# Pairwise products of 256 features: seven input places with refills and four output pieces per round, in place of a resident input and five

## The chip, the cores and the metric

One core of one Trainium2 chip. The metric is the device time of one execution in microseconds (us). The kernel before takes 1274.88 us, the median of 3 runs (1274.85 to 1274.91). The profile is of one execution, and its span (first to last instruction) is a little shorter, 1273.1 us.

## The reference

For every row of a batch of 4096 rows with 256 float32 features, all products of two features with i <= j are written, in the order of the upper triangle:

```python
# inputs: (4096, 256) float32
dot = jnp.einsum('bi,bj->bij', inputs, inputs)
iu, ju = jnp.triu_indices(256)
y = dot[:, iu, ju]            # (4096, 32896) float32
```

An output row has 256 x 257 / 2 = 32,896 columns, 131,584 bytes. The input is 4.19 MB, the output 538.97 MB. Row i of the triangle is a *run* of 256 - i columns: feature i times the features i to 255.

## The kernel before

128 partitions hold batch rows; a *round* is two batch rows per partition (256 rows in all), so there are 16 rounds. The whole input stays in SBUF (32 KB per partition). The columns of a round are cut into five pieces of about 6592 columns, each with an output buffer from a pool of three. ScalarE computes the first runs of a piece, one instruction per run and row; VectorE the others, both rows and often two neighbouring runs in one instruction. Two DMAs, one per row of the round, send the buffer out. The very first buffer goes out in four parts, so that the DMA gets work early.

```python
P = 128
UNIT = 64
REPEAT = 2
PIECES = 5
BUDGET = 0.95
FIRST = [512, 1536, 3584]
# ...
def vector_time(block: list) -> float:
    return sum(68 + 1.046 * REPEAT * n * m for (*_, n), m in vector_ops(block))
# ... split(): how many runs ScalarE takes, until VectorE's time is within BUDGET ns per element
    groups = n // (P * REPEAT)
    borders = even_borders(0, width, PIECES)
    slot = max(b - a for a, b in zip(borders, borders[1:]))

    xpool = ctx.enter_context(tc.tile_pool(name="x", bufs=1))
    opool = ctx.enter_context(tc.tile_pool(name="o", bufs=3))

    x_in = x.rearrange("(g p r) d -> p g (r d)", p=P, r=REPEAT)
    x_out = out.rearrange("(g p r) c -> g p r c", p=P, r=REPEAT)

    total = n // P * d
    xt = xpool.tile([P, total + 1], F32, name="x")
    nc.vector.memset(xt[:, total:], 0.0)
    cuts = [0, 1, groups // 2, groups]
    for a, b in zip(cuts, cuts[1:]):
        xs = xt[:, a * REPEAT * d : b * REPEAT * d]
        nc.sync.dma_start(xs.rearrange("p (g c) -> p g c", g=b - a), x_in[:, a:b])

    for g in range(groups):
        for c, (lo, hi) in enumerate(zip(borders, borders[1:])):
            o = opool.tile([P, REPEAT, slot], F32, tag="o", name=f"o_{g}_{c}")
            first = g == c == 0
            cuts = [lo, *(FIRST if first else []), hi]
            for a, b in zip(cuts, cuts[1:]):
                block = runs(d, a, b)
                k = split(block, 0.0 if first else BUDGET * REPEAT * (b - a))
                # ... ScalarE: block[:k], VectorE: block[k:]
                for r in range(REPEAT):
                    nc.sync.dma_start(x_out[g][:, r, a:b], o[:, r, a - lo : b - lo])
```

A VectorE instruction that takes two runs uses the length of the first for both, so its second run reads one element past its row: the first element of the next row in SBUF, which in the last row of a round belongs to the next round. What it writes there is overwritten by the next run.

In HBM, partition p of round g writes rows 256 g + 2 p and 256 g + 2 p + 1. Neighbouring partitions of one DMA are two rows apart.

Of the kernel before, what the change touches and what calls it, by code (L numbers as in the profile page):

```python
# [1 line left out]

# [4 lines left out]

F32 = mybir.dt.float32
AF = mybir.ActivationFunctionType
ALU = mybir.AluOpType  # L10

P = 128
UNIT = 64
REPEAT = 2
PIECES = 5
BUDGET = 0.95
FIRST = [512, 1536, 3584]


def even_borders(lo: int, hi: int, pieces: int) -> list[int]:  # L20
    units = (hi - lo) // UNIT
    return [lo + units * c // pieces * UNIT for c in range(pieces)] + [hi]


def runs(d: int, lo: int, hi: int) -> list:


    found, at = [], 0
    for i in range(d):
        a, b = max(at, lo), min(at + d - i, hi)  # L30
        if a < b:
            found.append((i, i + a - at, a, b - a))
        at += d - i
    return found


def vector_ops(block: list) -> list:

    ops, k = [], 0
    while k < len(block):
        i, j, at, n = block[k]
        m = 2 if k + 2 < len(block) and i == j else 1
        ops.append((block[k], m))
        k += m
    return ops


def interleave(block: list) -> list:


    half = len(block)
    while half and len(vector_ops(block[:half])) > len(vector_ops(block[half:])):
        half -= 1
    a, b = vector_ops(block[:half]), vector_ops(block[half:])
    return [op for k in range(max(len(a), len(b))) for ops in (a, b) for op in ops[k : k + 1]]


def vector_time(block: list) -> float:
    return sum(68 + 1.046 * REPEAT * n * m for (*_, n), m in vector_ops(block))


def split(block: list, budget: float) -> int:


    scalar, k = 0.0, 0
    while k < len(block):
        scalar += REPEAT * (184 + 0.837 * block[k][3])  # L70
        if vector_time(block[k:]) <= budget or scalar > vector_time(block[k + 1 :]):
            break
        k += 1
    return k


def window(ap: bass.AP, free: list) -> bass.AP:
    return bass.AP(ap.tensor, ap.offset, [list(ap.ap[0]), *free])


@with_exitstack
def kernel(
    ctx: ExitStack, tc: tile.TileContext, x: bass.AP, out: bass.AP
):

    nc = tc.nc  # L90
    n, d = x.shape
    width = out.shape[1]
    assert n % (P * REPEAT) == 0 and width == d * (d + 1) // 2 and width % UNIT == 0
# [4 lines that stand above are left out]
    xpool = ctx.enter_context(tc.tile_pool(name="x", bufs=1))  # L98
    opool = ctx.enter_context(tc.tile_pool(name="o", bufs=3))

    x_in = x.rearrange("(g p r) d -> p g (r d)", p=P, r=REPEAT)
    x_out = out.rearrange("(g p r) c -> g p r c", p=P, r=REPEAT)


    total = n // P * d
    xt = xpool.tile([P, total + 1], F32, name="x")
    nc.vector.memset(xt[:, total:], 0.0)  # L107
    cuts = [0, 1, groups // 2, groups]
    for a, b in zip(cuts, cuts[1:]):
        xs = xt[:, a * REPEAT * d : b * REPEAT * d]  # L110
        nc.sync.dma_start(xs.rearrange("p (g c) -> p g c", g=b - a), x_in[:, a:b])  # L111

    for g in range(groups):
        for c, (lo, hi) in enumerate(zip(borders, borders[1:])):
# [5 lines that stand above are left out]
                k = split(block, 0.0 if first else BUDGET * REPEAT * (b - a))  # L120
                for i, j, at, length in block[:k]:
                    for r in range(REPEAT):
                        row = (g * REPEAT + r) * d
                        nc.scalar.activation(  # L124
                            o[:, r, at - lo : at - lo + length],
                            xt[:, row + j : row + j + length],
                            AF.Copy,
                            scale=xt[:, row + i : row + i + 1],
                        )
                row = g * REPEAT * d  # L130
                for (i, j, at, length), m in interleave(block[k:]):
                    at -= lo
                    nc.vector.tensor_tensor(  # L133
                        o[:, :, at : at + m * length],
                        window(xt[:, row + j :], [[d, REPEAT], [1, m], [1, length]]),
                        window(xt[:, row + i :], [[d, REPEAT], [1, m], [0, length]]),
                        ALU.mult,
                    )
                for r in range(REPEAT):
                    nc.sync.dma_start(x_out[g][:, r, a:b], o[:, r, a - lo : b - lo])  # L140


# [1 line left out]
_INS = ["r_inputs"]  # L144
_OUTS = [((4096, 32896), "float32")]


# [20 lines left out]
```

## Time and profile before

| | |
|---|---|
| time | 1274.88 us (1274.85 to 1274.91) |
| span of the profiled execution | 1273.1 us |
| VectorE busy | 995.9 us (78%), 1813 instructions |
| ScalarE busy | 486.7 us (38%), 1547 instructions |
| DMA queue | 26,000 packets, 543.17 MB, 99.8% of 16 engines |
| output DMAs | 166, of which 128 have 3296 KB and 30 have 3264 KB |
| input DMAs | 3: 256, 1792 and 2048 KB |

A packet here is one partition's piece of one output row (up to 26,368 bytes) or one 2 KB stretch of input; each DMA also leaves one small completion packet on each of the 16 DMA engines. "Busy" of the DMA is the time that packets took, as a share of what 16 engines have in the span. An idle engine costs nothing if it is not the one that bounds the time.

### The profile page before, as it was taken

The numbers are of one execution on the slowest core, as the hardware profiler recorded it, in microseconds if no ns is written. First come the engines' busy times: TensorE is split into PE (matmuls) and PEld (weight loads), VectorE is DVE, ScalarE is ACT, GpSimd is POOL, SyncE is SP. The second block draws the span as 40 slices with busy tenths as digits, with TensorE's granted clock in tenths as the row PEclk, the third lists the DMA queues.
The fourth block names the chain that finished last, engine by engine and source line by source line (L and its number), as shares of the span: only waits on it lengthen the run. The fifth ranks groups of instructions, "written<-read, shape, count | busy, mean of one in ns | idle before, by whom it ended". The sixth has DMA issues, their size and how long they took to land.

```text
span 1273.1 us, 3975 instructions
## 1 busy us (share of the span) xinstructions
DVE 995.9 (78%) x1813; ACT 486.7 (38%) x1547; POOL 0.2 (0%) x4
## 2 busy tenths in 40 slices
DVE  8987887878778777787787787777777777777770
ACT  5523535234342343424334252342523425234250
POOL 0000000000000000000000000000000000000000
DMA  9999999999999999999999999999999999999998
GB/s 379 431 431 434 427 435 424 436 425 434 427 434 423 436 425 435 424 435 426 434 428 431 430 431 426 434 428 431 429 431 429 431 430 429 428 431 429 432 431 349
DMA packets 26031, 543.43 MB, mean 427 GB/s; under 512 B 2704, under 2 KB 2704, under 8 KB 5264
## 3 DMA queue, kind: packets, MB, share of 16 engines
q1 hardware_dynamic: 26000, 543.17, 99.8%
q14 instruction: 31, 0.25, 0.0%
HBM read 4.19 MB, written 538.97 MB: 427 GB/s over the span
## 4 chain that ended last, share of the span: by engine, by line
DMA 70%; DVE 25%; issue 1%; SPq 1%; DVEq 0%
DMA out_dram<-o 70%; DVE o L133 25%; SPq L140 1%; DMA x<-in_r_inputs_dram 1%; DVEq L133 0%; SPq L111 0%
## 5 line engine op out<-in xcount | busy, mean ns | idle before, releaser
L133 DVE TENSOR_TENSOR o<-x 128x356 f32<-128x356 f32 (+61 forms) x1812 | 995.8, 627 | 240.8 <-DMA out_dram<-o 191.4
L124 ACT ACTIVATE o<-x 128x253 f32<-128x253 f32 (+41 forms) x1546 | 485.4, 404 | 749.2 <-DMA out_dram<-o 722.3
L124 ACT ACT_TABLE_LOAD x1 | 1.3, 1283 | 0.7 <-PEq L155 0.7
L107 DVE MEMSET x<- 128x1 f32 x1 | 0.1, 59 | 0.8 <-PEq L155 0.8
L155 POOL MEMSET const-bfloat16-1.0<- 128x1 bf16 x1 | 0.1, 102 | 0.0
L155 POOL MEMSET const-uint8-127<- 128x1 uint8 x1 | 0.1, 102 | 0.0
L155 POOL MEMSET const-float32-0.0<- 128x1 f32 x1 | 0.1, 99 | 0.2 <-issue 0.2
L155 POOL MEMSET const-float32-1.0<- 128x1 f32 x1 | 0.1, 99 | 0.0
## 6 DMA issues: line engine op xcount, KB each, us to landing
out_dram<-o SPq DMA_DIRECT2D x128, 3296.0 KB, 27.2
out_dram<-o SPq DMA_DIRECT2D x30, 3264.0 KB, 28.8
out_dram<-o SPq DMA_DIRECT2D x2, 1472.0 KB, 13.0
x<-in_r_inputs_dram SPq DMA_DIRECT2D x1, 2048.0 KB, 13.4
out_dram<-o SPq DMA_DIRECT2D x2, 1024.0 KB, 9.7
x<-in_r_inputs_dram SPq DMA_DIRECT2D x1, 1792.0 KB, 8.2
out_dram<-o SPq DMA_DIRECT2D x2, 512.0 KB, 11.0
out_dram<-o SPq DMA_DIRECT2D x2, 256.0 KB, 10.5
```

Of the source, the lines that this page charges most:

```text
L107: nc.vector.memset(xt[:, total:], 0.0)
L124: nc.scalar.activation(o[:, r, at - lo : at - lo + length], xt[:, row + j : row + j + length], AF.Copy, scale=xt[:, row + i : row + i + 1],)
L133: nc.vector.tensor_tensor(o[:, :, at : at + m * length], window(xt[:, row + j :], [[d, REPEAT], [1, m], [1, length]]), window(xt[:, row + ...
L140: nc.sync.dma_start(x_out[g][:, r, a:b], o[:, r, a - lo : b - lo])
L155: nc = _bacc.Bacc("TRN2", target_bir_lowering=False, num_devices=1)
```

## The change

The partition now holds 32 adjacent batch rows of its own, in all rounds: partition p of round g has rows 32 p + 2 g and 32 p + 2 g + 1. Thus its input is one contiguous stretch per load. Only seven rounds have a place in SBUF at a time; after the first piece of rounds 3, 6 and 9, three more rounds are loaded into places whose rounds are done (at round 9 in two DMAs, as the places wrap around). The SBUF freed this way goes to the three output buffers, which grow from 6592 to 8224 columns, so that a round goes out in four pieces of 32,896 bytes per row. The unit of the cuts is 32 columns instead of 64, as 8224 is no multiple of 64. In HBM neighbouring partitions of one DMA are now 32 rows apart.

```diff
 P = 128
-UNIT = 64
+UNIT = 32
 REPEAT = 2
-PIECES = 5
+PIECES = 4
 BUDGET = 0.95
+AHEAD = 7
+LOADED = 3
 FIRST = [512, 1536, 3584]
@@
-    x_in = x.rearrange("(g p r) d -> p g (r d)", p=P, r=REPEAT)
-    x_out = out.rearrange("(g p r) c -> g p r c", p=P, r=REPEAT)
+    x_in = x.rearrange("(p r) d -> p (r d)", p=P)
+    x_out = out.rearrange("(p g r) c -> g p r c", p=P, r=REPEAT)
 
-    total = n // P * d
+    total = AHEAD * REPEAT * d
     xt = xpool.tile([P, total + 1], F32, name="x")
     nc.vector.memset(xt[:, total:], 0.0)
-    cuts = [0, 1, groups // 2, groups]
-    for a, b in zip(cuts, cuts[1:]):
-        xs = xt[:, a * REPEAT * d : b * REPEAT * d]
-        nc.sync.dma_start(xs.rearrange("p (g c) -> p g c", g=b - a), x_in[:, a:b])
+
+    def load(g: int, end: int):
+        while g < end:
+            place = g % AHEAD
+            m = min(end - g, AHEAD - place)
+            a, b, size = g * REPEAT * d, place * REPEAT * d, m * REPEAT * d
+            nc.sync.dma_start(xt[:, b : b + size], x_in[:, a : a + size])
+            g += m
+
+    load(0, 1)
+    load(1, AHEAD)
@@ (ScalarE and VectorE read the place of the round)
-                        row = (g * REPEAT + r) * d
+                        row = (g % AHEAD * REPEAT + r) * d
@@
-                row = g * REPEAT * d
+                row = g % AHEAD * REPEAT * d
@@ (after the two output DMAs of a piece)
+            if c == 0 and g and g % LOADED == 0 and g - LOADED + AHEAD < groups:
+                load(g - LOADED + AHEAD, min(g + AHEAD, groups))
```

## The prediction

> **What bounds the kernel now.** I read the page first: its slices, queues and chain.
>
> ```profile
> DMA  9999999999999999999999999999999999999998
> GB/s 379 431 431 434 427 435 424 436 425 434 427 434 423 436 425 435 424 435 426 434 428 431 430 431 426 434 428 431 429 431 429 431 430 429 428 431 429 432 431 349
> DMA packets 26031, 543.43 MB, mean 427 GB/s; under 512 B 2704, under 2 KB 2704, under 8 KB 5264
> ...
> q1 hardware_dynamic: 26000, 543.17, 99.8%
> ...
> DMA 70%; DVE 25%; issue 1%; SPq 1%; DVEq 0%
> ```
>
> The 16 DMA engines are busy 99.8% of the span and move about 430 GB/s in every slice but the first and the last. 543.17 MB at 430 GB/s is 1263 us of a span of 1273.1 us. The chain gives 25% to VectorE, but each of those stretches lies beside a full DMA queue, so I ask next who waits for whom.
>
> ```profile
> ACT o L124 <- DMA out_dram<-o: 722.3, 74, 12.7
> DVE o L133 <- DMA out_dram<-o: 191.4, 59, 4.0
> ```
>
> VectorE waits 191.4 us, in about 3 us pieces, for an output buffer to drain. One buffer takes it about 12.4 us (the chain in order of time) and takes the DMA 2 x 3296 KB / 430 GB/s = 15.7 us. Compute is ahead by 3.3 us per buffer; a faster VectorE buys nothing in the middle of the run. So the time is: the wait for the first packet, bytes and packets on the slowest DMA engine, any moment at which the DMA queue is empty, and the tail. The empty moments can only be at the start, so I looked at it in steps of 5 us and in order of time.
>
> ```profile
> 0.00:5.00 5.00, 1.40 (x5) 2.63 (x5) 0.20 (x4) 1.00 0.54 172
> 5.00:10.00 5.00, 3.57 (x8) 5.00 (x14) 0.00 (x0) 1.00 1.01 358
> 10.00:15.00 5.00, 5.00 (x7) 5.00 (x16) 0.00 (x0) 1.00 1.05 403
> 15.00:20.00 5.00, 5.00 (x7) 4.45 (x14) 0.00 (x0) 1.00 1.04 431
> 20.00:25.00 5.00, 5.00 (x6) 0.00 (x0) 0.00 (x0) 1.00 1.04 441
> 25.00:30.00 5.00, 5.00 (x8) 0.00 (x0) 0.00 (x0) 1.00 1.03 441
> ```
>
> The last two columns are the DMA share and GB/s. The DMA starts at about 2.1 us (issue at 0.73 us, so 1.4 us from issue to first packet) and is never empty again. This is not luck of the outputs alone: the queue holds all 4.19 MB of input first, some 11 us of work, and behind that cover the engines fill the first buffers.
>
> ```profile
> 3.66 4.28 DVE L133 TENSOR_TENSOR o<-x 128x512 f32<-128x512 f32 x9 [2.80 <-DMA x<-in_r_inputs_dram]
> 5.05 2.80 SPq L140 DMA_DIRECT2D out_dram<-o  x4
> 9.37 1.19 DVE L133 TENSOR_TENSOR o<-x 128x988 f32<-128x988 f32 x1 [1.43 <-DMA x<-in_r_inputs_dram]
> ...
> 12.55 1.09 SPq L140 DMA_DIRECT2D out_dram<-o  x2
> ...
> 15.74 1.07 SPq L140 DMA_DIRECT2D out_dram<-o  x2
> ...
> 28.03 0.81 SPq L140 DMA_DIRECT2D out_dram<-o  x2
> ```
>
> The first buffer goes out at 5.05 to 15.74 us in four parts, the second at 28.03 us. Bytes ahead of the second are 4.19 + 6.68 = 10.87 MB; with the measured rates they last until about 28.8 us. The cover is just long enough. At 9.37 us VectorE waits 1.43 us for the second input load: a product of two runs reads one element past its rows, the first of the next round.
>
> **What the Trainium skill says.** "DMA: Bandwidth & Descriptors", Where 436 GB/s comes from: 16 ports carry 435.2 GB/s. The trace's 430 is 99% of it, so larger pieces can win at most about 1%. Same page, Latency and other measured facts (row pitch): a pitch of 4 MiB between partitions halved the rate of copies, 4 MiB plus 4 KiB did not. The trace of before has a pitch of two rows, 263,168 bytes, at full rate; of a 4 MiB pitch no run here shows anything. Same page, How a descriptor splits into AXI transactions: a start off a 256-byte line costs part of one extra transaction. Same page, Queues, rings and completion order: each engine takes descriptors in ring order, so a refill waits behind the outputs issued before it and delays the later ones by its own length.
>
> **The change part by part.**
>
> 1. *Fewer, longer output packets.* The packet records of the trace have medians of 84 ns for 2048 bytes, 159 for 4096, 309 for 8192, 441 for 11,776, 973 for 26,112 and 981 for 26,368. The line through the 8192 and 26,368 bytes has 0.0370 ns per byte; what is not proportional to bytes is 6 to 14 ns a packet, depending on whether the median, the mean (983.7 ns) or the page's port rate is taken. I choose 11. Full pieces give 16 x 5 x 2 x 8 = 1280 packets per DMA engine before and 16 x 4 x 2 x 8 = 1024 after: 256 x 11 ns = 2.8 us less. 169 DMAs become 140, each with a 9 ns completion packet per engine: 0.3 us less. A packet of 32,896 bytes should take 1216 to 1223 ns.
> 2. *Input in longer packets.* Before, 2048 packets of 2 KB, 128 per engine, mean 91 ns (mixed with the first outputs of this size): 11.7 us. After, 8 packets per engine in each of six loads, 48 of 2 to 12 KB: at 0.037 ns per byte (262,144 bytes per engine) plus 48 x 11 ns, 10.2 us: 1.5 us less.
> 3. *Half of the pieces start off a 256-byte line in HBM* (8224 x 4 = 32,896 = 128.5 x 256). An estimate from the skill's section: a few ns on 512 packets per engine, 0 to 2 us; I take 0.5.
> 4. *Refills.* 9 of 16 rounds, 2.36 MB, are read within the run. By the builder's waits they hold up neither SyncE nor VectorE: the readers of those places are rounds back, and each refill is needed four rounds (some 300 us) later. Their bytes are in part 2; no wait is added.
> 5. *The start loses its cover.* Only 1.835 MB is queued up front. Going by before's rates it is in at about 7.5 us (landed 7.7), against 9.34 landed before for its first two loads. VectorE then resumes at 7.75 us. Parts 0 and 1 of the first buffer (1.35 and 2.5 us by packet times) keep the DMA busy to 11.4. Part 2 is ready 3.03 us of VectorE after 7.75 and issued at 10.9, its first packet comes 1.4 us later, 12.3: gap 0.9. It lasts 16 x 309 ns = 4.9 us, to 17.2. Part 3 is now 4640 columns instead of 2944: seven VectorE instructions, 6.2 us by the kernel's own formula, 68 ns + 1.046 ns per element, which fits before's 3.2 us between the issues at 12.55 and 15.74. Issued 17.1, first packet 18.5: gap 1.3. 16 packets of 695 ns last to 29.6. The second buffer needs 15.3 us of VectorE (before: 12.3, as 15.74 to 28.03 shows): issued 32.4, first packet 33.8: gap 4.2. It then lasts 19.5 us, to 53.3, and the third, ready at 48, is in time; from there compute is ahead by 19.5 - 15.5 = 4 us per buffer. Sum of the gaps: 6.4 us that before does not have.
>
> Sum: -2.8 - 0.3 - 1.5 + 0.5 + 6.4 = +2.3 us: span about 1275.4, time about 1277.
>
> **The rivals.** *The longer packets win more, the gaps less* (1269 to 1273): possible if the 430 is held down by packet ends that queue at the ports; for it speaks that 2 KB packets run at 403 and 26 KB at 430. Against: the rise is nearly used up at 26 KB, and the skill's ceiling leaves 1.2%. *The new pitch of 32 rows costs HBM rate* (1300 to beyond 1400): 32 x 131,584 = 4,210,688 bytes, 4 MiB + 16 KiB. The pad is larger than the 4 KiB that sufficed in the skill's figures, so I hold it for safe, but nothing in the trace tests it: 7%. *The refills stall something* (+10 to 30 us): if compute after a refill waited for it, it would wait for two queued buffers, some 35 us, three times; the waits as built don't show that. *VectorE becomes the bound*: 995.9 us busy, 3.3 us of slack per buffer; its work is unchanged. No.
>
> **Range and chances.** Mechanical uncertainty is about 3 us for packets and 2 us for gaps; the misaligned starts and the pitch stretch the upper side. Range 1270 to 1287. Faster by over 2% (under 1249.4) would need more than the port ceiling: 1%. Slower by over 2% (over 1300.4) only by pitch or stall: 7%.
>
> **What would show it.** In the slices of the first 60 us, DMA share falls below 9 near 12, 18 and above all 30 to 34 us; second buffer issued near 32 us; steady rate 430 to 432 GB/s; packets about 20,200; VectorE's wait for output about 4 us a time. A steady rate under 422 would mean pitch or alignment; dips after rounds 3, 6 and 9 would mean the refills; no dip near 32 us would make step 5 wrong.

## The result

The kernel after takes 1284.09 us (1284.05 to 1284.25), against 1274.89 us before: ratio 1.0072, 95% interval 1.0055 to 1.0090. It is 9.2 us slower; the prediction's sum was 2.3 us (about 1277 us).

The page of the kernel after, the same parts as shown of before:

```profile
DMA  7999999999999999999999999999999999999996
GB/s 320 426 427 427 435 433 427 428 414 434 435 429 431 435 432 422 430 431 437 429 430 435 431 419 430 435 429 432 435 430 431 433 431 428 436 430 427 435 433 274
DMA packets 20189, 543.41 MB, mean 424 GB/s; under 512 B 2240, under 2 KB 2240, under 8 KB 3392
...
q1 hardware_dynamic: 20160, 543.17, 98.8%
...
DMA 69%; DVE 26%; SPq 1%; ACT 0%; issue 0%; DVEq 0%; ACTq 0%
```

The middle of the run is as before: some 430 GB/s with a fifth fewer packets. What differs are the two ends. The first slice fell from 379 to 320 GB/s, the last from 349 to 274. Each slice is 32 us, so these are (379 - 320) / 430 x 32 = 4.4 us and (349 - 274) / 430 x 32 = 5.6 us of DMA time.

The start, in steps of 5 us; the last two columns are the DMA share and GB/s:

```profile
0.00:5.00 5.00, 1.78 (x5) 3.00 (x6) 0.20 (x4) 1.00 0.67 247
5.00:10.00 5.00, 4.31 (x9) 5.00 (x14) 0.00 (x0) 1.00 0.98 385
10.00:15.00 5.00, 5.00 (x7) 5.00 (x15) 0.00 (x0) 1.00 0.82 338
15.00:20.00 5.00, 5.00 (x7) 5.00 (x15) 0.00 (x0) 1.00 0.85 354
20.00:25.00 5.00, 5.00 (x6) 3.49 (x11) 0.00 (x0) 1.00 1.01 431
25.00:30.00 5.00, 5.00 (x7) 0.06 (x1) 0.00 (x0) 1.00 0.69 297
30.00:35.00 5.00, 5.00 (x8) 5.00 (x18) 0.00 (x0) 1.00 0.51 212
```

And its issues in order of time: eight for the first buffer's four parts, then none until the second buffer at 32.27 us.

```profile
4.67 13.08 SPq L150 DMA_DIRECT2D out_dram<-o  x8
...
32.27 35.87 SPq L150 DMA_DIRECT2D out_dram<-o  x6
```

VectorE is nearly full from 5 us on, yet the DMA share dips three times, at 10 to 15, 15 to 20 and most at 25 to 35 us. The packet records have three gaps in which no engine moves anything, 0.55, 1.0 and 4.0 us, 5.6 us in all; before has none. These are the gaps of step 5 of the prediction.

Now the other end, for which the prediction had no number. Before:

```profile
1260.00:1265.00 5.00, 0.00 (x0) 0.00 (x0) 0.00 (x0) 1.00 0.99 427
1265.00:1270.00 5.00, 0.00 (x0) 0.00 (x0) 0.00 (x0) 1.00 0.41 174
1270.00:1275.00 5.00, 0.00 (x0) 0.00 (x0) 0.00 (x0) 1.00 0.02 11
```

After:

```profile
1260.00:1265.00 5.00, 0.00 (x0) 0.00 (x0) 0.00 (x0) 1.00 0.99 428
1265.00:1270.00 5.00, 0.00 (x0) 0.00 (x0) 0.00 (x0) 1.00 0.81 349
1270.00:1275.00 5.00, 0.00 (x0) 0.00 (x0) 0.00 (x0) 1.00 0.18 79
1275.00:1280.00 5.00, 0.00 (x0) 0.00 (x0) 0.00 (x0) 1.00 0.14 59
```

A share of 0.18 is three of 16 engines. Thirteen are done by about 1271 us; three go on for 6 to 10 us more, and the kernel waits for the last.

Each DMA leaves one landing per engine, so the landing records split every run's time in two: when the median engine lands its part of the last DMA (counted from about the first packet; I call it *the typical engine*), and how much later the last one does (*the lag*). Before: 1265.5 and 5.0. After: 1268.4 and 11.3. The typical engine is 2.9 us later, the lag 6.3 us longer: together the 9.2 us. All runs are read this way below, each from one traced execution. The point from which the typical engine is counted is good to some 0.2 us from run to run; the lag does not depend on it.

### The profile page after: what moved, and what is told of

It reads as the page before. It is cut to its first block, busy times and chain, and to the rows that moved or that the text cites. A ratio compares the mean times of both kernels' runs of the same rounds, so it can differ in the third digit from the quotient of the medians.

```text
span 1282.3 us, 3770 instructions
## 1 busy us (share of the span) xinstructions
DVE 989.1 (77%) x1812; ACT 471.6 (37%) x1453; POOL 0.2 (0%) x4
## 4 chain that ended last, share of the span: by engine, by line
DMA 69%; DVE 26%; SPq 1%; ACT 0%; issue 0%; DVEq 0%; ACTq 0%
DMA out_dram<-o 68%; DVE o L143 26%; SPq L150 1%; DMA x<-in_r_inputs_dram 0%; ACT o L134 0%; DVEq L143 0%; SPq L117 0%; ACTq L134 0%
## 5 line engine op out<-in xcount | busy, mean ns | idle before, releaser
L143 DVE TENSOR_TENSOR o<-x 128x4 f32<-128x4 f32 (+59 forms) x1811 | 989.0, 624 | 248.3 <-DMA out_dram<-o 233.5
L134 ACT ACTIVATE o<-x 128x253 f32<-128x253 f32 (+45 forms) x1452 | 470.3, 415 | 763.2 <-DMA out_dram<-o 755.5
```

The costliest lines, as they stand in the source:

```text
L134: nc.scalar.activation(o[:, r, at - lo : at - lo + length], xt[:, row + j : row + j + length], AF.Copy, scale=xt[:, row + i : row + i + 1],)
L143: nc.vector.tensor_tensor(o[:, :, at : at + m * length], window(xt[:, row + j :], [[d, REPEAT], [1, m], [1, length]]), window(xt[:, row + ...
```

## The experiments

| run | time, us | ratio to before (95% interval) | typical engine, us | lag, us |
|---|---|---|---|---|
| before | 1274.9 | | 1265.5 | 5.0 |
| after | 1284.09 | 1.0072 (1.0055 to 1.0090) | 1268.4 | 11.3 |
| no_refill | 1276.43 | 1.0012 (1.0005 to 1.0019) | 1262.7 | 9.6 |
| start_shared | 1280.40 | 1.0043 (1.0028 to 1.0058) | 1264.9 | 11.1 |
| rows_as_before | 1285.75 | 1.0084 (1.0067 to 1.0101) | 1269.0 | 12.2 |
| unit64 | 1282.14 | 1.0057 (1.0042 to 1.0072) | 1268.2 | 9.5 |
| refill_by_one | 1282.20 | 1.0057 (1.0042 to 1.0072) | 1268.2 | 9.9 |
| after_mended | 1278.29 | 1.0027 (1.0017 to 1.0037) | 1264.9 | 9.2 |
| five_pieces | 1282.77 | 1.0060 (1.0043 to 1.0077) | 1269.4 | 9.1 |
| late_input | 1275.66 | 1.0006 (0.9997 to 1.0015) | 1266.1 | 6.2 |
| layout_only | 1274.24 | 0.9994 (0.9986 to 1.0003) | 1264.4 | 5.6 |
| few_instr | 1274.81 | 0.9998 (0.9990 to 1.0007) | 1265.6 | 5.1 |
| four_plain | 1268.21 | 0.9947 (0.9932 to 0.9962) | 1259.3 | 4.8 |
| five_plain | 1270.32 | 0.9963 (0.9950 to 0.9976) | 1261.4 | 4.7 |

The trace of late_input is of its slowest execution, 1276.55 us; those of the other runs lie within 0.2 us of the time given.

### no_refill: the kernel after without its refills

```diff
-            if c == 0 and g and g % LOADED == 0 and g - LOADED + AHEAD < groups:
-                load(g - LOADED + AHEAD, min(g + AHEAD, groups))
```

Rounds 7 to 15 multiply whatever their place holds; the reading of 2.36 MB is left out.

> The kernel after without its refills: rounds 7 to 15 multiply what lies in the seven places from the start, so 2.36 MB of input are never read and their products are of the wrong rows. Theory A (the 9.2 us are 6.3 us of empty DMA queue at the start, and the rest is what the refills cost beyond their bytes, because reads and writes that meet in one DMA engine slow each other and the slowest engine sets the end): the bytes alone are worth 5.7 us, the disturbance another 3 to 5 us, so 1284.1 becomes 1274 to 1275.5 us, and the DMA engines finish closer together. Theory B (the rest is the new place of rows in HBM, or the starts off a 256-byte line): the bytes alone go, 1278.4 us.

1276.43 us, 7.7 us less than after: between the two theories. The typical engine gains 5.7 us, about what the bytes were expected to be worth. The other 2.0 us are beyond the bytes; the lag is 1.7 us shorter. What a refill does is seen at the first one, in steps of 5 us. After:

```profile
265.00:270.00 5.00, 1.16 (x4) 0.00 (x0) 0.00 (x0) 1.00 0.98 305
```

and without refills:

```profile
265.00:270.00 5.00, 1.17 (x5) 0.25 (x1) 0.00 (x0) 1.00 1.04 447
```

The engines are nearly as busy (0.98) but move 305 GB/s. The packet records have 15 output packets of 1.7 to 2.3 us there in place of 1.22, and one 6 KB read of 2.18 us where the median is 0.234; such clusters stand at the three times of refills (266, 503 and 739 us) and at none of them in no_refill. At 430 GB/s the missing bytes are 1.5 us.

### start_shared: more work for ScalarE in the first two buffers

```diff
-FIRST = [512, 1536, 3584]
+FIRST = [512, 1536, 3584, 5632]
-                k = split(block, 0.0 if first else BUDGET * REPEAT * (b - a))
+                k = split(block, 0.0 if g == 0 and c < 2 else BUDGET * REPEAT * (b - a))
```

> The kernel after, with the first buffer cut at 5632 columns as well and the second buffer's work shared evenly between VectorE and ScalarE. Theory A: the gaps of 1.3 and 4.2 us in the DMA queue before 34 us vanish, the one of 0.9 us stays: 1284.1 becomes 1278.5 to 1279.5 us. If the end is set by something that the start does not delay (a rival: the lag of the slowest DMA engine is caught up with anyway), it stays above 1282.

1280.40 us, 3.7 us less, about 1 us short of what Theory A expected: a gap of 0.9 us was left where it had none. Time with no packet fell from 5.6 to 1.5 us, so 4.1 us of gap were worth 3.7. The gap is on the path; little of it is caught up later. The lag stayed (11.1).

### rows_as_before: the rows of before in the kernel after

```diff
-    x_in = x.rearrange("(p r) d -> p (r d)", p=P)
-    x_out = out.rearrange("(p g r) c -> g p r c", p=P, r=REPEAT)
+    x_in = x.rearrange("(g p r) d -> p g (r d)", p=P, r=REPEAT)
+    x_out = out.rearrange("(g p r) c -> g p r c", p=P, r=REPEAT)
@@ (in load: the same rounds, one 2 KB stretch per round)
```

> The kernel after with the batch rows where before had them (neighbouring partitions two rows apart in HBM, input in 2 KB packets). Theory A: the place of rows does not matter; the longer read packets are lost, at most 1.5 us more: 1284 to 1286 us. Theory B (pitch): packets of 32,896 bytes get shorter, 1279 to 1281 us.

1285.75 us: 1.7 us more, as the shorter read packets would have it. No cost of the pitch of 4 MiB + 16 KiB shows; Theory B's pitch has fallen. It agrees with the Trainium skill ("DMA: Bandwidth & Descriptors", Latency and other measured facts), where copies at a 4 MiB pitch were back at full rate once it was padded by 4 KiB.

### unit64: every piece starts on a 256-byte line

```diff
-UNIT = 32
+UNIT = 64
```

The pieces are 8192 and 8256 columns.

> The kernel after with cuts at multiples of 64 columns: pieces of 8192 and 8256 columns, every piece starting on a 256-byte line of HBM. Theory A: 1284 us, within 1. Theory B (starts off the line): 1280 to 1281 us, and the packet records lose the part that is above 1218 ns.

1282.14 us, 1.95 us less, and not where I looked: the typical engine gains 0.2 us, the lag 1.8. The packets did not get shorter in the median: 1213 and 1222 ns for 32,768 and 33,024 bytes, 1218 for 32,896. The last engines fell less far behind. The run moves three things at once: the starts of every second piece and the ends of the others in HBM, and the place of the second row within its SBUF buffer, all come to multiples of 256 bytes. No run separates them; "starts off the line" below stands for the three together.

### refill_by_one: nine small refills

```diff
-            if c == 0 and g and g % LOADED == 0 and g - LOADED + AHEAD < groups:
-                load(g - LOADED + AHEAD, min(g + AHEAD, groups))
+            if c == 0 and g and g - 1 + AHEAD < groups:
+                load(g - 1 + AHEAD, g + AHEAD)
```

> The kernel after with nine refills of one round each (256 KB, 2 KB packets, after the first piece of rounds 1 to 9) in place of three of three rounds. If the disturbance goes by the meetings of reads and writes: three times the 2 us, so about 1288 us. If it goes by bytes: 1284 to 1285 us. If short reads between writes disturb less: under 1284.

1282.20 us, 1.9 us *less*. The disturbance does not go by the number of meetings: nine short reads disturb less than three long ones. Whether the size of a read (256 against 768 KB) or of its packets (2 against 6 KB) does it, the run can't tell.

### late_input: input late in the kernel before (a miss)

```diff
-    cuts = [0, 1, groups // 2, groups]
-    for a, b in zip(cuts, cuts[1:]):
+    load(0, 1)
+    load(1, 7)
@@ (after the output DMAs of a piece)
+            if g == 3 and c == 0:
+                load(7, groups)
```

> The kernel before with one thing changed: rounds 7 to 15 of the input are read after the first piece of round 3 instead of at the start (same places, same five pieces, rows and packets). Theory A (input read at the start was free, as it lay where the outputs were not ready): the DMA queue is empty for 5 to 6.5 us before the second buffer goes out at 28 us, and the one late read disturbs the outputs for about 1 us: 1274.9 becomes 1280 to 1282 us. Rival (the start does not matter, the longer span comes from the size of the pieces or the rows): within 1 us of before.

1275.66 us, only 0.7 us more; the interval reaches 1. But the run did not do what its expectation says. The program's order in time:

```profile
4.89 2.77 SPq L143 DMA_DIRECT2D out_dram<-o  x4
7.71 0.91 SPq L111 DMA_DIRECT2D x<-in_r_inputs_dram  x1
```

Nothing in the program forced the late read to be late (its places are free from the start), and it was issued at 7.7 us, right after the first two parts. So it covered the gap after all, and no moment without packets is recorded. It shows only that in this kernel input which joins the queue by 7.7 us still covers the start. The question went to the next run.

### five_pieces: the kernel after with the pieces of before

```diff
-UNIT = 32
-PIECES = 4
+UNIT = 64
+PIECES = 5
```

> The kernel after, seven places and refills and its rows kept, but with the five pieces of before (cuts at multiples of 64 columns). Theory A (the queue runs empty because too little input is queued ahead of the first outputs): the second buffer still comes at about 27 to 28 us, the queue is empty some 5 us before it, refills disturb for 2 us: about 1281 us. Theory D (the queue runs empty mainly because the pieces are longer, so that the second buffer comes at 32 us): the gap is 2 us or less and the time is 1276 to 1278 us.

1282.77 us: 7.9 of the 9.2 us are there with the pieces of before. Its start, in steps of 5 us:

```profile
10.00:15.00 5.00, 5.00 (x9) 5.00 (x16) 0.00 (x0) 1.00 0.80 326
15.00:20.00 5.00, 5.00 (x7) 4.34 (x13) 0.00 (x0) 1.00 1.03 431
20.00:25.00 5.00, 5.00 (x6) 0.37 (x2) 0.00 (x0) 1.00 0.74 311
25.00:30.00 5.00, 5.00 (x8) 5.00 (x17) 0.00 (x0) 1.00 0.60 255
...
4.94 22.27 SPq L150 DMA_DIRECT2D out_dram<-o  x10
```

The last line has the ten issues of the first two buffers, from 4.94 to 27.21 us; the second buffer's two begin at 26.40 us, even earlier than the 28.03 of before. Yet the queue is empty for 4.0 us. Theory A stands over Theory D: the loss of cover makes most of the gap (4.0 of 5.6 us), the longer pieces add 1.6. Against before, the typical engine is 3.9 us later (about the gap) and the lag 4.1 us longer; here every piece starts on the line, so this is put down to the refills.

### layout_only: the new rows in the kernel before

```diff
-    x_in = x.rearrange("(g p r) d -> p g (r d)", p=P, r=REPEAT)
-    x_out = out.rearrange("(g p r) c -> g p r c", p=P, r=REPEAT)
+    x_in = x.rearrange("(p r) d -> p (r d)", p=P)
+    x_out = out.rearrange("(p g r) c -> g p r c", p=P, r=REPEAT)
@@ (each of the three loads one contiguous stretch per partition)
```

> The kernel before with the new place of rows alone: each partition has 32 adjacent rows, input resident, in three loads with packets of 2, 14 and 16 KB, five pieces. Theory A: reads are shorter by about 1.5 us and the start stays covered: 1273.4 to 1274.9 us. Theory B (pitch of 32 rows costs): above 1277 us.

1274.24 us, 0.7 us less; the interval reaches 1. The typical engine gained 1.1 us. No harm from the pitch, here either: the stretch from 100 to 1200 us has 430 GB/s.

### few_instr: fewer instructions in the kernel before

The lag has visible steps of 0.5 to 0.8 us at the times at which the trace has an 8 KB instruction fetch. That made a theory, C. The records do not name the engine of a packet or of a fetch.

```diff
-                k = split(block, 0.0 if first else BUDGET * REPEAT * (b - a))
+                k = split(block, 0.0 if first else (1.1 if g else BUDGET) * REPEAT * (b - a))
```

> The kernel before with less work for ScalarE from round 1 on (budget 1.1 instead of 0.95): VectorE gets some 14.3 us of work per buffer instead of 12.4, still under the 15.7 us of the DMA, and there are some 550 instructions fewer, so about 4 fewer fetches of 8 KB of instructions. Theory C (three DMA engines lag at the end because the fetches of instructions go through them, about 0.7 us each): 1.0 to 2.0 us faster than before, and the slowest engines' lag shrinks. Rival (the lag has another cause): within 0.4 us of before.

1274.81 us, no difference, lag 5.1. The instructions did get fewer; the page counts the fetch packets, 26 in place of before's 31:

```profile
q14 instruction: 26, 0.21, 0.0%
```

The gain that Theory C forecast did not come. But the run took away only five of 31 fetches, and the landing records still tie the lag to them. Take the three engines that land last, add up how far they are behind the typical one, and look from 60 us on. In before this sum grows by 22.3 us over the 26 DMAs in which a fetch falls, and shrinks by 11.8 us over the 128 others: the three fall behind at fetches, some 0.8 us each, and catch up in between. Here it is 19.5 and -9.8; the three end 3.8 us behind on average instead of 4.3, but the last of them 5.1, and the time goes by the last.

The run also shows VectorE's slack: 1138.9 us busy instead of 995.9, at no cost.

### four_plain and five_plain: the length of the packets alone

Both are start_shared without refills and with `UNIT = 64` (rounds 7 to 15 on old places, as in no_refill); the second has `PIECES = 5` and the FIRST of before.

```diff
 # five_plain against four_plain
-PIECES = 4
+PIECES = 5
-FIRST = [512, 1536, 3584, 5632]
+FIRST = [512, 1536, 3584]
```

> To measure the length of the packets by itself: no refills (rounds 7 to 15 multiply what lies in the seven places, so their products are of the wrong rows), cuts at multiples of 64 columns, shared start, four pieces. To be compared with the run five_plain. If the parts found so far add: 1276.4 - 3.7 - 2.0 = 1270.7 us.

> As four_plain (no refills, wrong rows in rounds 7 to 15, shared start) but with five pieces. If 256 fewer packets per DMA engine are worth their overhead of 8.6 ns each: 2.2 to 2.8 us slower than four_plain. If the slowest engines' lag grows with longer packets and eats that (the lag at the end was 5 us in before and 9 to 11 us with four pieces): equal, or faster than four_plain.

1268.21 and 1270.32 us: longer packets win 2.1 us, and the lag is the same (4.8 and 4.7). So longer packets do what they are for (2.1 us over 256 packets per engine is about 8 ns for each packet saved), and do not by themselves make engines lag. Four_plain's end:

```profile
1255.00:1260.00 5.00, 0.00 (x0) 0.00 (x0) 0.00 (x0) 1.00 0.98 423
1260.00:1265.00 5.00, 0.00 (x0) 0.00 (x0) 0.00 (x0) 1.00 0.17 73
1265.00:1270.00 5.00, 0.00 (x0) 0.00 (x0) 0.00 (x0) 1.00 0.00 0
```

beside that of no_refill, where half of the pieces start off the line:

```profile
1260.00:1265.00 5.00, 0.00 (x0) 0.00 (x0) 0.00 (x0) 1.00 0.78 336
1265.00:1270.00 5.00, 0.00 (x0) 0.00 (x0) 0.00 (x0) 1.00 0.14 59
1270.00:1275.00 5.00, 0.00 (x0) 0.00 (x0) 0.00 (x0) 1.00 0.05 20
```

Here is what single removals had hidden. The three mends taken one by one are worth 7.7 + 3.7 + 1.95 = 13.3 us; all together 15.9. With refills only (unit64, five_pieces, after_mended) the lag is 9.1 to 9.5; with starts off the line only (no_refill) 9.6; with both 9.9 to 12.2; with neither 4.7 to 5.6. Each alone nearly doubles the lag, so removing only one shows little of it. Taken away where the other is gone already, each is worth more: the refills 1278.29 - 1268.21 = 10.1 us, of which 5.7 are their bytes, so 4.4 beyond them instead of 2.0; the starts 1276.43 - 3.7 - 1268.21 = 4.5 us instead of 1.95 (the 3.7 for the start, if that adds).

The sum taken under few_instr shows where this comes from. At fetches it grows by 16 to 25 us in every kernel here. Over all other DMAs it shrinks by 9 to 13 us in the kernels with neither source, moves by -1 to +3 us with one, and grows by 4 to 10 us with both. (Late_input, with one read among its first outputs, is in between: -5.4.) So the two sources do not bring more steps; they take away the catching up. That is read from the records; no run tests why.

### after_mended: the parts together, with the whole output

The kernel after with start_shared's start, `UNIT = 64` and few_instr's budget.

> The kernel after with three changes: cuts at multiples of 64 columns, the start shared between the engines (as in the run start_shared), and budget 1.1 from round 1 on (fewer instructions). If the parts add: 1284.1 - 3.7 - 2.0 - 1.5 = 1276.9 us, 1276 to 1278. If the lag of the slowest engine eats what the start gives back: 1279 or more.

1278.29 us. Without the 1.5 us for instructions, which few_instr shows to be nothing, the sum is 1278.4: the parts add. It takes back 5.8 of the 9.2 us and remains slower than before. Its lag is 9.2: the refills remain, and without them four_plain has 4.8. No version here with the whole output is clearly faster than before.

## Why the prediction was right and where it was not

1277 us was predicted, 1270 to 1287 as the range; 1284.1 lies in its upper half. The direction and the first mechanism were right, the forecast change was a quarter of the measured one. That 1284.1 falls into the range is partly luck: its upper side was left open for the pitch, which cost nothing, and for the starts off the line, which cost something of another kind; nothing in it stood for engines that fall behind.

- *Step 1, packets, -2.8 us and -0.3.* Right in kind, but a third of the 3.1 us did not come: 2.1 us between the two plain runs, some 8 ns a packet instead of 11. (The 8.6 ns in the expectation of five_plain is no better: packet medians of 26 and 33 KB move by 3 to 6 ns with the run and the stretch that are taken, which is as much as the thing to be found.)
- *Step 2, reads, -1.5 us.* Right in sign: 1.7 us in rows_as_before; in layout_only 0.7 by time, which is not clear of noise, and 1.1 on the typical engine.
- *Step 3, starts off the line, 0.5 us.* Mis-sized: 1.95 us, and almost none of it where the step put it. It is not a few ns on every packet but a few engines falling behind.
- *Step 4, refills, "no wait is added".* True, and not enough. SyncE has no wait for input at all, and VectorE's two (the line below) are those of the start. But the DMA engines' rate falls to 305 GB/s while reads meet writes: 2.0 us beyond the bytes when the refills alone are removed, 4.4 when the starts are on the line.

```profile
DVE o L143 <- DMA x<-in_r_inputs_dram: 3.1, 2, 2.4
```

- *Step 5, the gaps, +6.4 us.* Upheld almost to the number: second buffer issued at 32.27 us (predicted 32.4), dips at the three places, gaps of 0.55, 1.0 and 4.0 us (predicted 0.9, 1.3 and 4.2). Removing 4.1 of the 5.6 us gave 3.7 back.

The sum, +2.3 us, holds for the typical engine, which is 2.9 us later, in part because the gaps and the savings were both put too high. The step that failed is the one from there to the end: the path was taken to be a typical engine's, and it is the last engine's. The prediction named "bytes and packets on the slowest DMA engine" and "the tail" as parts of the time, then reckoned with one packet for all engines and gave the tail no number. The last window of before, share 0.41 and then 0.02, would have shown that the end is set by a few engines up to 5 us behind the rest. What the sum lacked is the growth of that lag, 5.0 to 11.3 us. Its sources are shown by removal: the refills and the starts off the line, each enough to bring it above 9. The rival "the refills stall something" was near in its object and wrong in its kind; the pitch had no part.

Open: why three engines and not the others; why refills and starts off the line keep these from catching up; which of the three things that unit64 moves matters. That the lag begins at fetches of instructions is read from the records, not shown by a run: fewer of them gave no time, and after has fewer than before (29 against 31), so their number is not what grew. Reads on a queue of their own were not tried.

## What to carry to other kernels

The DMA queue bounds this kernel, and input read up front was not a cost in it but the cover under which the first outputs are made. Before freeing such space, count the bytes ahead of each of the first outputs against the time at which these are ready. Take the end of a kernel like this from its slowest DMA engine, not from the mean: look at the DMA share of the last 10 us first. Larger transfers won just their overhead per packet (2.1 us of 1270); two side effects of making room for them, reads among the writes and starts off the 256-byte line, cost about as much each when removed singly, and over 4 us each when the other was gone. And where two causes hide each other, remove both before calling either small.

## What the runs showed of the hardware that I had not expected

- Three of 16 DMA engines end 3.6 to 5.0 us after the others even in the kernel before, and 7 to 11 us in the one after; they lose it bit by bit over the whole run.
- In no_refill a fetch of 8 KB of instructions takes 0.31 us, and in 14 cases an output packet that starts as a fetch ends takes 1.70 us in place of 1.22: together the 0.8 us by which the last engines fall behind at a fetch.
- 768 KB of reads among writes brought the rate from 447 to 305 GB/s for 5 us at a busy share of 0.98; 256 KB at a time was cheaper in all (1282.2 against 1284.1 us).
- Starts and ends at an odd multiple of 128 bytes left the typical engine's time as it was (within 0.2 us) and still cost 1.95 us.
- A pitch of 4 MiB + 16 KiB between the partitions of a store ran at the rate of before, 430 GB/s.
